# Row maxima of the second attention in pieces of 512 keys, and who adds the weights

## The chip, the cores and the metric

The kernel runs on one core of one Trainium2 chip. The metric is the device time of one execution in microseconds (us); lower is better. The engines of the core are named as in the profile: PE (TensorE, matmuls), PEld (its weight loads), DVE (VectorE), ACT (ScalarE), POOL (GpSimd) and SP (SyncE, which issues DMAs).

## The reference

`x` is 4 x 512 tokens of 256 features and `ctx_1024` is 4 x 1601 context rows of 256 features. Two layers follow each other, each an attention over the context and then a feed-forward part with eight experts. Everything is float32.

```python
x = x + _L0_xattn_ref(ctx_1024, _layernorm(x), ...)      # 8 heads of 128, over context and x
x = x + _L0_ffn_ref(_layernorm(x), ...)                  # 2 of 8 experts a token, limited capacity
x = x + _L1_xattn_ref(ctx_1024, _layernorm(x), Wq, Wk, Wv, 1, 0, 1)
x = x + _L1_ffn_ref(_layernorm(x), ...)                  # 2 of 8 experts a token
```

The third line is what the change touches. It has 8 heads of 32 features, 512 queries and 1601 keys in each of four batches:

```python
q = _split_heads(query @ Wq.T, h)     # query: the normalized x
k = _split_heads(key @ Wk.T, h)       # key, value: the context
v = _split_heads(value @ Wv.T, h)
attn = jnp.einsum('bhnd,bhmd->bhnm', q, k) * scale
attn = jax.nn.softmax(attn, axis=-1)
x = jnp.einsum('bhnm,bhmd->bhnd', attn, v)
```

## The kernel before

The kernel works in four stages, one behind the other: first attention, first experts, second attention, second experts. The second attention is cut into 16 units. A unit `u` is one batch `b`, one group `o` of four heads (`HG` is 4) and one half `f` of the queries, 256 of them. The 1601 keys of a unit make 13 key tiles (`NM`), 12 of 128 keys and one of 65.

A softmax needs the maximum of each row of scores before its exponentials. The kernel therefore computes the scores twice, in two layouts:

- `maxima(u, g)` has queries on the partitions and keys along the row. One call takes 128 queries and a quarter of the keys (400 or 401, `edges`), for all four heads. It takes two tiles of the PSUM pool `ps_s`, writes the scores of two heads into each (L1133), and VectorE reduces each tile to its maxima `tops` (L1141). There are eight calls to a unit: two groups of queries times four quarters.
- `negated(u)` (L1150) reduces `tops` to one negative maximum for each query and head, in `shift`; `to_row(u)` turns it (L1163, PE) and ScalarE copies it as an extra row beside the queries, in `asked` (L1167).
- `weights(u, j)` has the 128 keys of tile `j` on the partitions and queries along the row. Four matmuls (L1180) give the scores, less the maxima through that extra row, in one tile of `ps_s`; ScalarE takes the exponential (L1193) into `pT`.
- `add_weights(u, j, pT)` (L1202) adds that tile to a running sum of the unit. There are two sums. The tiles `j` in `by_pool` are added by GpSimd, the others by VectorE. The first tile of each sum is written by ScalarE straight into the sum's buffer.
- `weigh(u, j, pT, ps)` (L1211) multiplies the weights with the values. `closing` (L1230 on) adds the two sums over the keys, divides and adds the result to `x`.

The loop at the end of the stage takes two key tiles a step and runs over the key tiles of all 16 units, so that steps cross from one unit to the next (13 is odd). The maxima of unit `u` are computed some 18 key tiles ahead, within the steps of the unit before. A step of the kernel before issues, in this order: one call of `maxima` if one is due, `weights` of two key tiles, further calls of `maxima` if due, then `add_weights` and `weigh` for the two tiles of the previous step (`held`), and last what the table `at` has for these key tiles: `negated`, `to_row`, loads of queries and keys, projections for the next batch, layer norms, routing for the second experts. `in_order` ties the instructions of PE, DVE, ACT and POOL to the order in which the program issues them; nothing reorders them. The DMA queue of SP takes its loads as they are issued.

The pools matter here. `ps_s` has three buffers of two PSUM banks each, handed out in turn: whoever asks for a buffer waits until the tile handed out three requests earlier has been read. `pT` has six buffers. With `ps_o` and `ps_m`, one buffer each, this fills the eight banks.

Of the kernel before, what the change touches and what calls it, by code (L numbers as in the profile page):

```python
# [8 lines left out]
F32 = mybir.dt.float32  # L9
# [7 lines left out]
P = 128  # L17
B, S, D = 4, 512, 256
M = 1601
# [9 lines left out]
NM = -(-M // P)  # L29
# [7 lines left out]
H1, DH1 = 8, 32  # L37
HG = P // DH1
# [29 lines left out]
def xattn_ffn_twice(ctx: ExitStack, tc: tile.TileContext, a: dict, out: bass.AP):  # L68
    nc = tc.nc

    @contextmanager
    def in_order(*engines):

        block = nc.cur_bb.bb
        start = len(block.instructions)
        yield
        assert nc.cur_bb.bb is block
        last = {}
        for k, ins in enumerate(block.instructions):
            if ins.engine not in {e.engine for e in engines}:  # L80
                continue
            if k >= start and ins.engine in last:
                tc.add_manual_dep(
                    ins,
                    last[ins.engine].name,
                    mybir.DependencyInfo(
                        mybir.DependencyClass.NoSync, mybir.DependencyReason.DATA
                    ),
                    reason="in_order",
                )  # L90
            last[ins.engine] = ins
# [440 lines left out]
    with ExitStack() as st:  # L532
# [3 lines left out]
        two = st.enter_context(tc.tile_pool(name="a_two", bufs=2))  # L536
# [167 lines left out]
        def values(pair, part):  # L704

            blocks = parts[part]
            v = one.tile([P, len(blocks), 2 * DH0], F32, tag=f"v{part}", name=f"v{part}")
            cols = slice(INNER + pair * 2 * DH0, INNER + (pair + 1) * 2 * DH0)  # L710

            def some(j0):
                n = min(2, len(blocks) - j0)
                ps = ps_t.tile([P, 2, 2 * DH0], F32, tag="t", name="ps_v")
                for k in range(n):
                    j = blocks[j0 + k]
                    for c in range(DC):
                        nc.tensor.matmul(  # L718
                            ps[:, k, :],
                            lhsT=flat_kvin[c][:, j * P : (j + 1) * P],  # L720
                            rhs=wkv[:, c, cols],
                            start=c == 0,
                            stop=c == DC - 1,
                        )
                nc.scalar.copy(v[:, j0 : j0 + n, :], ps[:, :n, :])  # L725

            return v, [lambda j0=j0: some(j0) for j0 in range(0, len(blocks), 2)]
# [72 lines left out]
        for h in range(H0):  # L800
            nc.vector.tensor_copy(values_bias, bqk[:, 2, h : h + 1].to_broadcast([P, P]))
            nc.tensor.matmul(
                ps, lhsT=values_bias, rhs=wo[:, h, :], start=h == 0, stop=h == H0 - 1
# [21 lines left out]
        for n in range(n_steps + 4):  # L825
            b, h, t = n // (H0 * NT), n // NT % H0, n % NT
            if n < n_steps:
                if t == 0:
# [3 lines left out]
                    g = n // NT + 1  # L832
# [5 lines left out]
                if t >= 2 and h % 2 == 0:  # L838
                    v, f = values(h // 2, t - 2)
# [18 lines left out]
            if 1 <= n <= n_steps:  # L858
                p = (n - 1) // 2
# [9 lines left out]
            pieces = []  # L869
# [3 lines left out]
            p = (n - 3 - part) // 2  # L873
# [43 lines left out]
    def keys_values(psum, tag, b, evacuate=evacuate):  # L917


        cT = w1p.tile([P, DC, M], F32, tag="cT", name="cT")  # L920
        nc.sync.dma_start(cT, a["ctxT"][b].rearrange("(c p) m -> p c m", p=P))
        kT = [kv1.tile([P, M], F32, tag=f"kT{o}", name=f"kT{o}") for o in range(DC)]
        v = kv1.tile([P, NM, D], F32, tag="v1", name="v1")

        def some_keys(o, j0):
            n = min(512, M - j0)
            ps = psum.tile([P, 512], F32, tag=tag, name="ps_k1")
            for c in range(DC):
                nc.tensor.matmul(
                    ps[:, :n],  # L930
                    lhsT=wT[:, 1, c, o * P : (o + 1) * P],
                    rhs=cT[:, c, j0 : j0 + n],
                    start=c == 0,
                    stop=c == DC - 1,
                )
            evacuate(kT[o][:, j0 : j0 + n], ps[:, :n])

        def some_values(j0):
            n = min(2, NM - j0)
            ps = psum.tile([P, 2, D], F32, tag=tag, name="ps_v1")  # L940
            r = P
            for k in range(n):
                r = rows_of(j0 + k, NM, TAIL)
                for c in range(DC):
                    nc.tensor.matmul(
                        ps[:r, k, :],
                        lhsT=cT[:, c, (j0 + k) * P : (j0 + k) * P + r],
                        rhs=wT[:, 2, c, :],
                        start=c == 0,
                        stop=c == DC - 1,  # L950
                    )
            evacuate(v[:r, j0 : j0 + n, :], ps[:r, :n, :])

        steps = [lambda j0=j0: some_keys(0, j0) for j0 in range(0, M, 512)]
        steps += [lambda j0=j0: some_values(j0) for j0 in range(0, NM, 2)]
        steps += [lambda j0=j0: some_keys(1, j0) for j0 in range(0, M, 512)]
        return kT, v, steps

    def run(kvs):
        for s in kvs[2]:  # L960
            s()
        return kvs[:2]
# [30 lines left out]
    with ExitStack() as st:  # L993
        two = st.enter_context(tc.tile_pool(name="b_two", bufs=2))
# [11 lines left out]
        kvs = [run(keys_values(ps_h, "h", 0))]  # L1006
# [41 lines left out]
    QH = 2 * P  # L1048
    with ExitStack() as st:
        one = st.enter_context(tc.tile_pool(name="c_one", bufs=1))  # L1050
        two = st.enter_context(tc.tile_pool(name="c_two", bufs=2))
# [46 lines left out]
        qTs = {}  # L1098
# [17 lines left out]
                        qTs[b][i * DH1 : (i + 1) * DH1, o, f * QH : (f + 1) * QH],  # L1116
                    )

        edges = [k * M // HG for k in range(HG + 1)]
        tops = {}  # L1120

        def maxima(u, g):

            b, o, f = units[u]
            t, k = divmod(g, HG)
            if g == 0:
                tops[u] = two.tile([P, 2, HG, HG], F32, tag="tops", name="tops")
            lo, hi = edges[k], edges[k + 1]
            q0 = f * QH + t * P
            pss = [ps_s.tile([P, 2, 512], F32, tag="s", name=f"ps_s{i}") for i in range(2)]  # L1130
            for i in range(HG):
                rows = slice(i * DH1, (i + 1) * DH1)
                nc.tensor.matmul(  # L1133
                    pss[i // 2][:, i % 2, : hi - lo],
                    lhsT=qTs[b][rows, o, q0 : q0 + P],
                    rhs=kvs[b][0][o][rows, lo:hi],
                    start=True,
                    stop=True,
                )
            for pair in range(2):  # L1140
                nc.vector.tensor_reduce(  # L1141
                    tops[u][:, t, 2 * pair : 2 * pair + 2, k],
                    pss[pair][:, :, : hi - lo],
                    AX.X,
                    ALU.max,
                )
# [20 lines left out]
                nc.scalar.copy(asked[u % 3][r : r + 1], ps[r : r + 1])  # L1167


        by_pool = (1, 3, 5, 7, 9, 11)  # L1170
        sums = {}

        def weights(u, j):
# [93 lines left out]
        at = {}  # L1267
# [64 lines left out]
        load_queries(0)  # L1332
        load_keys(0, 1)
        ordered = st.enter_context(in_order(*computing))
        for g in range(2 * HG):
            maxima(0, g)
        negated(0)
        to_row(0)

        ahead = {}  # L1340
        for u in range(1, n_units):
            for g in range(2 * HG):
                step = NM * u - 5 - NM + (g * NM) // (2 * HG)
                ahead.setdefault(max(step, 0) // 2, []).append((u, g))

        held = []
        for step in range(0, NM * n_units + 10, 2):
            first, *more = ahead.pop(step // 2, [None])
            if first:
                maxima(*first)  # L1350
            fresh = []
            for k in range(step, step + 2):
                u, j = divmod(k, NM)
                if u < n_units:
                    fresh.append((u, j, weights(u, j)))
            for g in more:
                maxima(*g)
            for h in held:
                add_weights(*h)
            for uw, jw, pT in held:  # L1360
                if jw == 0:
                    ps_of = ps_o.tile([P, QH], F32, tag="o", name="ps_o1")
                weigh(uw, jw, pT, ps_of)
                if jw == NM - 1:
                    ending = closing(uw, ps_of)
                    next(ending)
                    put(step + 4, lambda ending=ending: next(ending))
                    put(step + 6, lambda ending=ending: next(ending, None))
            for k in range(step, step + 2):
                for f in at.pop(k, []):  # L1370
                    f()
            held = fresh
# [5 lines left out]
    with ExitStack() as st:  # L1378
        one = st.enter_context(tc.tile_pool(name="d_one", bufs=1))
        two = st.enter_context(tc.tile_pool(name="d_two", bufs=2))  # L1380
# [224 lines left out]
        rest = routing()  # L1605
        fetched = [first_tile(0), first_tile(1)]
        more = [lambda e=e: first_tile(e) for e in range(2, E)]
# [41 lines left out]
        with tc.If(ties > 0):  # L1649
            for b in range(B):  # L1650
                for t0 in range(0, NT, GR):
                    rows, acc = [], spare.tile([P, GR, D], F32, tag="acc", name="acc")
# [18 lines left out]
                    for e in range(E):  # L1671
                        t = spare.tile([P, WIDE], F32, tag="w", name="w_t")
# [83 lines left out]
```

## Time and profile before

| | |
|---|---|
| median of 3 runs | 3014.13 us (3011.76 to 3015.57) |
| profiled execution | 3014.63 us, span 3012.6 us, mean granted clock 0.965 |
| busy shares of the span | PE 92%, DVE 48%, ACT 31%, POOL 16% |
| second attention, main loop | about 1985 to 2680 us of the span |
| maxima, reductions L1141 | 256, mean 984 ns |
| weights, scores L1180 | 1664 matmul records |
| weights, exponentials L1193 | 1023 ns each |
| sums on DVE L1202 | 96, mean 1597 ns |
| sums on POOL L1202 | 80, mean 2463 ns |

A row of a group names line, engine, operation, tiles (output <- inputs), shapes and count; then busy time in us, mean ns of one, and the time that the engine stood idle just before such instructions, with what ended it. In a timeline a row has start in us, duration in us, engine, line and operation; in brackets stands the idle time before it and what ended it. Each float32 matmul of the program appears as two records. The ends of matmuls are modelled, so the distance from one start to the next says more than the duration.

### The profile page before, as it was taken

How to read it: one execution, taken by the hardware profiler on the slowest of the kernel's cores; microseconds unless marked ns; L12 is line 12 of the kernel's file. 1: busy time of each engine (PE TensorE's matmuls, PEld its weight loads, DVE VectorE, ACT ScalarE, POOL GpSimd, SP SyncE). 2: the span in 40 equal slices, each digit the busy share in tenths (PEclk: the TensorE clock that was granted, in tenths of full speed). 3: DMA queues.
4: the chain of work that ended last, by engine and by line, in shares of the span. 5: the costliest groups of instructions: out<-in, count | busy, mean ns of one | idle time of the engine just before them, and what ended most of it. 6: DMA issues, size and time to landing. Idle time of an engine off the chain costs nothing. (4 is left out here: it accounts for less than half of the span.)

```text
span 3012.6 us, 35574 instructions
## 1 busy us (share of the span) xinstructions
PE 2781.7 (92%) x13426; PEld 1846.2 (61%) x13426; DVE 1444.5 (48%) x2324; ACT 931.1 (31%) x1312; POOL 473.7 (16%) x340
## 2 busy tenths in 40 slices
PE   5699999999999999999997999788988888898998
PEld 2466676666666667666665566544444444467887
DVE  4256447554476444464444100177775757751110
ACT  2233234232343333332321212123433434341221
POOL 1000000100001000010000100122424434343442
PEclk9899999999999999999998999889999999999999
DMA  8743334433343333333334233210101110045652
GB/s 297 234 123 94 99 92 105 112 96 92 94 113 104 98 86 95 93 102 97 92 96 148 93 98 105 66 27 14 30 26 36 30 35 22 13 172 165 193 171 73
DMA packets 165103, 295.95 MB, mean 98 GB/s; under 512 B 43287, under 2 KB 81752, under 8 KB 161848
## 3 DMA queue, kind: packets, MB, share of 16 engines
q1 hardware_dynamic: 124024, 204.45, 24.2%
q0 software_dynamic: 16320, 53.42, 5.9%
q10 hardware_dynamic: 24576, 35.68, 4.6%
q8 instruction: 109, 1.79, 0.3%
q14 instruction: 74, 0.61, 0.1%
HBM read 97.86 MB, written 49.76 MB: 49 GB/s over the span
## 5 line engine op out<-in xcount | busy, mean ns | idle before, releaser
L743 DVE TENSOR_REDUCE top<-ps_s 128x1 f32<-128x2113 f32 x128 | 301.8, 2358 | 578.9 <-PE ps_s L735 578.9
L772 PE MATMUL ps_o<-pT,v 128*128 128x256 f32 x2176 | 520.9, 381 | 7.8 <-DVE pT L764 7.8
L735 PE MATMUL ps_s<-kT,qT 128*128 128x512 f32 (+1 forms) x1280 | 489.0, 527 | 26.7 <-ACT attn L749 26.3
L772 PEld LDWEIGHTS ps_o<-pT,v 128*128 128x128 f32 x2176 | 410.9, 191 | 124.8 <-issue 69.9
L735 PEld LDWEIGHTS ps_s<-kT,qT 128*128 128x128 f32 x1280 | 241.5, 191 | 276.3 <-issue 239.9
L749 ACT ACTIVATE attn<-ps_s,top 128x2113 f32<-128x2113 f32 x128 | 258.9, 2023 | 486.1 <-DVE top L743 411.5
L764 DVE STREAM_TRANSPOSE pT<-swapped 128x2176 f32<-128x2176 f32 x128 | 312.4, 2441 | 70.2 <-DMA swapped<-attn 59.4
L1141 DVE TENSOR_REDUCE tops<-ps_s 128x2 f32<-128x800 f32 (+1 forms) x256 | 241.0, 984 | 150.7 <-PE ps_s L1133 150.6
L1180 PE MATMUL ps_w<-asked,keyed 64*128 64x256 f32 (+1 forms) x1664 | 243.7, 418 | 45.7 <-DVE tops L1141 39.4
L685 PE MATMUL ps_k<-kvin,wkv 128*128 128x512 f32 (+1 forms) x640 | 261.9, 533 | 5.2 <-ACT kT L692 5.2
L718 PE MATMUL ps_v<-wkv,kvin 128*128 128x256 f32 x1088 | 253.5, 381 | 0.0
L1202 POOL TENSOR_TENSOR sum<-sum,pT 128x1024 f32<-128x1024 f32 x80 | 197.0, 2463 | 334.4 <-ACT pT L1193 243.5
L1180 PEld LDWEIGHTS ps_w<-asked,keyed 64*128 64x128 f32 (+1 forms) x1664 | 150.4, 193 | 155.6 <-DVE tops L1141 79.7
L1193 ACT ACTIVATE pT<-ps_w 128x1024 f32<-128x1024 f32 (+1 forms) x176 | 178.2, 1023 | 195.4 <-PE ps_w L1180 191.8
L718 PEld LDWEIGHTS ps_v<-wkv,kvin 128*128 128x128 f32 x1088 | 204.9, 190 | 32.7 <-issue 3.4
L692 ACT ACTIVATE kT<-ps_k,bqk 128x512 f32<-128x512 f32 (+1 forms) x160 | 97.1, 620 | 268.1 <-DMA swapped<-attn 128.8
L685 PEld LDWEIGHTS ps_k<-kvin,wkv 128*128 128x128 f32 x640 | 116.5, 192 | 81.0 <-issue 67.1
L1202 DVE TENSOR_TENSOR sum<-sum,pT 128x1024 f32<-128x1024 f32 x96 | 153.3, 1597 | 6.2 <-ACT pT L1193 3.0
L725 ACT COPY v<-ps_v 128x512 f32<-128x512 f32 x144 | 79.8, 560 | 226.2 <-PE ps_v L718 154.0
L1445 PE MATMUL ps_h<-xT,w_e 128*128 128x256 f32 x640 | 143.7, 383 | 3.7 <-issue 3.7
L1133 PE MATMUL ps_s<-kT,qT 32*128 32x400 f32 (+1 forms) x1024 | 142.1, 582 | 3.2 <-ACT pT L1193 2.6
L1464 PE MATMUL ps_y<-w_e,hT 128*128 128x256 f32 x640 | 144.4, 385 | 0.0
(261 smaller groups left out, 2635.6 us busy)
## 6 DMA issues: line engine op xcount, KB each, us to landing
swapped<-attn SPq DMA_DIRECT2D x1536, 68.0 KB
swapped<-attn ACTq DMA_DIRECT2D x512, 68.0 KB
rows_b<-empty SPq DMA_DIRECT2D x36, 530.0 KB
w<-in_w_dram SPq DMA_DIRECT2D x16, 1024.0 KB
w_e<-in_wall_dram SPq DMA_DIRECT2D x7, 2052.0 KB
cT<-in_ctxT_dram SPq DMA_DIRECT2D x4, 1601.0 KB
keyed<-kT SPq DMA_DIRECT2D x32, 200.1 KB
ctx_b<-in_ctx_dram SPq DMA_DIRECT2D x4, 1536.0 KB
```

Source lines behind the costliest of these rows:

```text
L685: nc.tensor.matmul(ps[:, :n], lhsT=wkv[:, c, hs], rhs=flat_kvin[c][:, j0 : j0 + n], start=c == 0, stop=c == DC - 1,)
L718: nc.tensor.matmul(ps[:, k, :], lhsT=flat_kvin[c][:, j * P : (j + 1) * P], rhs=wkv[:, c, cols], start=c == 0, stop=c == DC - 1,)
L735: nc.tensor.matmul(flat[:, j0 : j0 + n], lhsT=qT[:, t * P : (t + 1) * P], rhs=kT[:, j0 : j0 + n], start=True, stop=True,)
L743: nc.vector.tensor_reduce(top, flat[:, :L], AX.X, ALU.max, negate=True)
L749: nc.scalar.activation(attn[:, :L], flat[:, :L], AF.Exp, bias=top, accum_out=total)
L764: nc.vector.transpose(pT[:, :, k * P : (k + 1) * P].rearrange("p c (a i) -> p a c i", a=4), swapped.rearrange("p a (c i) -> p a c i", i=32),)
L772: nc.tensor.matmul(ps, lhsT=v[:, j - parts[part][0], (h % 2) * DH0 : (h % 2 + 1) * DH0], rhs=pT[:, j, :], start=j == 0, stop=j == NB - 1,)
L1141: nc.vector.tensor_reduce(tops[u][:, t, 2 * pair : 2 * pair + 2, k], pss[pair][:, :, : hi - lo], AX.X, ALU.max,)
L1180: nc.tensor.matmul(ps[:r, s, pair * QH : (pair + 1) * QH], lhsT=keyed[o][64 * s : 64 * s + 64, pair, j * P : j * P + r], rhs=asked[u % 3][ ...
L1193: nc.scalar.activation(pT[:r], ps[:r], AF.Exp)
L1202: (nc.gpsimd if k else nc.vector).tensor_tensor(to, to, pT[:r], ALU.add)
L1464: nc.tensor.matmul(ps, lhsT=hT[:, f, r * P : (r + 1) * P], rhs=w(WB1 + f * D, D), start=f == 0, stop=f == FC - 1,)
```

## The change

The four quarters of the keys become three pieces of 512 keys, for each of the two groups of 128 queries, and one last piece that holds the remaining 65 keys of both groups side by side. That makes seven calls of `maxima` a unit instead of eight, with the same number of matmuls and of scores; the last call's reduction gives both groups' maxima at once. `tops` keeps its shape, four values a query and head.

In a step, all calls of `maxima` that are due now stand between the scores of the first and of the second key tile; none stands ahead of the first. They are due every second key tile.

GpSimd's tiles become `j` = 1, 4, 7, 10 in place of 1, 3, 5, 7, 9, 11. As the first of each only starts a sum, GpSimd now makes three of the eleven additions of a unit and VectorE eight; before they made five and six.

```diff
-        edges = [k * M // HG for k in range(HG + 1)]
+        rest = M // 512 * 512
+        pieces = [[(t, j0, 512)] for t in range(2) for j0 in range(0, rest, 512)]
+        pieces.append([(t, rest, M - rest) for t in range(2)])
+        n_tops = rest // 512 + 1
         def maxima(u, g):
             b, o, f = units[u]
-            t, k = divmod(g, HG)
...
-            lo, hi = edges[k], edges[k + 1]
-            q0 = f * QH + t * P
             pss = [ps_s.tile([P, 2, 512], F32, tag="s", name=f"ps_s{i}") for i in range(2)]
-            for i in range(HG):
-                rows = slice(i * DH1, (i + 1) * DH1)
-                nc.tensor.matmul(
-                    pss[i // 2][:, i % 2, : hi - lo],
-                    lhsT=qTs[b][rows, o, q0 : q0 + P],
-                    rhs=kvs[b][0][o][rows, lo:hi],
...
+            at = 0
+            for t, j0, n in pieces[g]:
+                q0 = f * QH + t * P
+                for i in range(HG):
+                    rows = slice(i * DH1, (i + 1) * DH1)
+                    nc.tensor.matmul(
+                        pss[i // 2][:, i % 2, at : at + n],
+                        lhsT=qTs[b][rows, o, q0 : q0 + P],
+                        rhs=kvs[b][0][o][rows, j0 : j0 + n],
...
+                at += n
+            t, j0, n = pieces[g][0]
             for pair in range(2):
+                of = pss[pair][:, :, :at].rearrange("p i (t n) -> p t i n", n=n)
                 nc.vector.tensor_reduce(
-                    tops[u][:, t, 2 * pair : 2 * pair + 2, k],
-                    pss[pair][:, :, : hi - lo],
+                    tops[u][:, t : t + at // n, 2 * pair : 2 * pair + 2, j0 // 512],
+                    of,
...
-        by_pool = (1, 3, 5, 7, 9, 11)
+        by_pool = (1, 4, 7, 10)
...
-                step = NM * u - 5 - NM + (g * NM) // (2 * HG)
+                step = NM * u - 6 - NM + 2 * g
                 ahead.setdefault(max(step, 0) // 2, []).append((u, g))
         for step in range(0, NM * n_units + 10, 2):
-            first, *more = ahead.pop(step // 2, [None])
-            if first:
-                maxima(*first)
             fresh = []
             for k in range(step, step + 2):
                 u, j = divmod(k, NM)
                 if u < n_units:
                     fresh.append((u, j, weights(u, j)))
-            for g in more:
-                maxima(*g)
+                if k == step:
+                    for g in ahead.pop(step // 2, ()):
+                        maxima(*g)
             for h in held:
                 add_weights(*h)
```

More of the change, by code (lines that the diff above doesn't have):

```diff
@@ L1117, in load_queries @@
                     )
-        edges = [k * M // HG for k in range(HG + 1)]
+        rest = M // 512 * 512
+        pieces = [[(t, j0, 512)] for t in range(2) for j0 in range(0, rest, 512)]
+        pieces.append([(t, rest, M - rest) for t in range(2)])
+        assert 2 * (M - rest) <= 512
+        n_tops = rest // 512 + 1
         tops = {}
@@ L1124, in maxima @@
             b, o, f = units[u]
-            t, k = divmod(g, HG)
             if g == 0:
-                tops[u] = two.tile([P, 2, HG, HG], F32, tag="tops", name="tops")
-            lo, hi = edges[k], edges[k + 1]
-            q0 = f * QH + t * P
+                tops[u] = two.tile([P, 2, HG, n_tops], F32, tag="tops", name="tops")
             pss = [ps_s.tile([P, 2, 512], F32, tag="s", name=f"ps_s{i}") for i in range(2)]
-            for i in range(HG):
-                rows = slice(i * DH1, (i + 1) * DH1)
-                nc.tensor.matmul(
-                    pss[i // 2][:, i % 2, : hi - lo],
-                    lhsT=qTs[b][rows, o, q0 : q0 + P],
-                    rhs=kvs[b][0][o][rows, lo:hi],
-                    start=True,
-                    stop=True,
-                )
+            at = 0
[7 more added lines that the diff above has]
+                        rhs=kvs[b][0][o][rows, j0 : j0 + n],
+                        start=True,
+                        stop=True,
+                    )
+                at += n
+            t, j0, n = pieces[g][0]
             for pair in range(2):
+                of = pss[pair][:, :, :at].rearrange("p i (t n) -> p t i n", n=n)
                 nc.vector.tensor_reduce(
-                    tops[u][:, t, 2 * pair : 2 * pair + 2, k],
-                    pss[pair][:, :, : hi - lo],
+                    tops[u][:, t : t + at // n, 2 * pair : 2 * pair + 2, j0 // 512],
+                    of,
                     AX.X,
@@ L1334, in xattn_ffn_twice @@
         ordered = st.enter_context(in_order(*computing))
-        for g in range(2 * HG):
+        for g in range(len(pieces)):
             maxima(0, g)
@@ L1341, in xattn_ffn_twice @@
         for u in range(1, n_units):
-            for g in range(2 * HG):
-                step = NM * u - 5 - NM + (g * NM) // (2 * HG)
+            for g in range(len(pieces)):
+                step = NM * u - 6 - NM + 2 * g
                 ahead.setdefault(max(step, 0) // 2, []).append((u, g))
```

## The prediction

> **What bounds the kernel now.** I read first the busy shares by stretch, cut to the second attention (1985 to 2680 us, 16 units), since the diff touches nothing else; then the costliest groups; then the waits of TensorE; then the timeline of a plain step. Nothing is saturated in that stage, as the sum over the stretches shows (695 us):
>
> ```profile
> sum 695.00, PE 599.66 PEld 322.36 DVE 491.35 ACT 281.35 POOL 284.12; mean PE 42.83 PEld 23.03 DVE 35.10 ACT 20.10 POOL 20.29
> ```
>
> TensorE (PE) is nearest to full, with 95 us idle, and VectorE (DVE) is at 71%. The page gives the durations of what the change touches:
>
> ```profile
> L1141 DVE TENSOR_REDUCE tops<-ps_s 128x2 f32<-128x800 f32 (+1 forms) x256 | 241.0, 984 | 150.7 <-PE ps_s L1133 150.6
> L1202 POOL TENSOR_TENSOR sum<-sum,pT 128x1024 f32<-128x1024 f32 x80 | 197.0, 2463 | 334.4 <-ACT pT L1193 243.5
> L1202 DVE TENSOR_TENSOR sum<-sum,pT 128x1024 f32<-128x1024 f32 x96 | 153.3, 1597 | 6.2 <-ACT pT L1193 3.0
> ```
>
> The waits of TensorE in the stage (us, times, longest) name the reduction first:
>
> ```profile
> PE ps_w L1180 <- DVE tops L1141: 39.4, 33, 4.9
> PE ps_c L468 <- DVE earlier L464: 16.7, 3, 5.6
> PE ps_r L1163 <- DVE shift L1150: 15.2, 8, 3.0
> ```
>
> The timeline of a plain step shows why: maxima (M), scores of two key tiles (W0, W1), values of the two tiles before (G).
>
> ```profile
> 2112.28 0.96 PE L1133 MATMUL ps_s<-kT,qT 32*128 32x401 f32 x8
> ...
> 2113.17 2.29 PE L1180 MATMUL ps_w<-asked,keyed 64*65 64x256 f32 x16
> 2113.27 1.89 DVE L1141 TENSOR_REDUCE tops<-ps_s 128x2 f32<-128x802 f32 x2 [2.42 <-PE ps_s L1133]
> ...
> 2114.32 0.73 PEld L1180 LDWEIGHTS ps_w<-asked,keyed 64*128 64x128 f32 x8 [0.53 <-DVE tops L1141]
> ...
> 2115.38 1.07 PE L1211 MATMUL ps_o<-pT,v 128*32 128x256 f32 x16
> ...
> 2116.38 0.95 PE L1133 MATMUL ps_s<-kT,qT 32*128 32x400 f32 x8
> ```
>
> Start to start, M is 0.89 us, W0 with W1 2.21, G 1.00: 4.10 a step. `ps_s` has three buffers and M takes two, so W1 reuses the first buffer of the M just before it, and starts only when that reduction ends (2113.27 + 0.98 = 2114.25, then 2114.32). In the last unit, where no maxima are left, W0 and W1 take 1.88 to 1.93. So even the best step loses 0.3 us there, and any lateness of VectorE is passed on in full. The worst plain case is a step with two maxima (three in 13):
>
> ```profile
> 2100.28 1.14 PE L1180 MATMUL ps_w<-asked,keyed 64*128 64x256 f32 x8 [1.19 <-DVE tops L1141]
> 2101.35 0.95 PE L1133 MATMUL ps_s<-kT,qT 32*128 32x400 f32 x8
> ...
> 2102.34 1.89 DVE L1141 TENSOR_REDUCE tops<-ps_s 128x2 f32<-128x800 f32 x2 [1.21 <-PE ps_s L1133]
> 2102.69 2.34 POOL L1202 TENSOR_TENSOR sum<-sum,pT 128x1024 f32<-128x1024 f32 x1 [3.65 <-ACT pT L1193]
> 2104.14 1.97 DVE L1202 TENSOR_TENSOR sum<-sum,pT 128x1024 f32<-128x1024 f32 x1
> ...
> 2106.25 0.66 PE L1163 MATMUL ps_r<-ident,shift 128*128 128x128 f32 x4 [2.95 <-DVE shift L1150]
> ```
>
> **What the Trainium skill says.** "SBUF — State Buffer", Who interferes with whom: VectorE with two SBUF inputs and a reading GpSimd exclude each other for a whole instruction; a reduction is never affected. The trace agrees: the addition at 2104.14 lasts 1.97 us because GpSimd's runs to 2105.04, others last 1.21, while reductions stay between 923 and 996 ns. "TensorE: Matmul & The Clock Gate", What's actually happening: the clock halves after idle windows of about 3.4 us. In the stage's stretches PEclk means 0.936, so some 89 us ran at half clock, costing about 44. "TensorEngine Tiling", Key Properties: a change of tiling mode drains the array. M, W and G have three modes, and the new order W M W G has four changes a step for three; no row prices one alone.
>
> **The change part by part.** Times are from W0's start.
>
> *Sizes.* A reduction of 1,024 elements: L1141 gives 984 ns at 800 and L743 2358 at 2113, so 1.046 ns an element and 1.22 us; the piece of 260 comes to 0.42. Per unit 12 x 1.22 + 2 x 0.42 = 15.5 us against 16 x 0.984 = 15.7: nothing, and the 16 reductions of the prologue likewise. Matmuls: L685 at 512 columns costs 261.9/640 = 409 ns, L718 at 256 costs 253.5/1088 = 233, so 0.69 ns a column; M of 512 is 0.89 + 2 x 112 x 0.69 ns = 1.04 us. The last piece, 16 short instructions, is unseen: between 0.3 (by columns) and 0.9 (by count); I take 0.5.
>
> *Order.* W0 [0, 0.96], M [0.96, 2.0]. W1 now reuses W0's buffer, so it needs ScalarE's exponential: scores start to exponential start is 1.18 in the timeline (2117.27 to 2118.45), plus 1.02, plus 0.06 to start: W1 at 2.26, 0.26 later than TensorE could. W1 takes 1.06 (2114.32 to 2115.38), G 1.00: a step of 4.32. Reductions start at 2.1; issued behind each other they take 1.13 each (the pair above takes 1.89 for 2 x 0.98), so they end at 4.5. Who waits: the next W0 (at 4.32) needs the first, done at 3.3; the next M (at 5.28) needs the second, done at 4.5. VectorE may be about 0.8 us late at no cost, where it now may not be late at all. Per 13 steps (two units, 16 maxima before, 14 after, one step holding two): before 10 x 4.10 + 3 x 4.99 = 56.0; after 13 x 4.32 + 1.0 = 57.2. Eight pairs: **+10 us**.
>
> *Waits removed.* After a two-maxima step VectorE does four reductions and an addition (3.6 + 1.13) from 1.0 on, with a gap for the second matmuls, so it is free at about 7.0 and the next W1 starts 0.9 us late: 24 such steps, **-22**. The ps_o wait of GpSimd's second sum (j=3 comes two steps after j=1, whose matmul still reads that buffer) makes it collide with VectorE and TensorE then loses about 2.3 us in each of three batches; with j=4 it is not late: **-7**. Of some 45 us by which the timeline's W1 and M come late at full clock, these leave 16, which follow layer-norm and collecting work on VectorE; the new slack takes half, **-8**. The wait for `shift` (15.2 us, 8 times): the new step has one M, and VectorE ends reductions, an addition and `shift` at 5.9 against G's end at 4.3, so 1.6 a time: **-2**.
>
> *Sums.* GpSimd 80 to 48, VectorE 96 to 128. Unblocked 1.21 each: +39 us of VectorE, less about a third of the 36 us (96 x 0.38) now lost to the lock: 491 to some 520 of 695, and a step holds 2.26 + 1.23 x 1.13 = 3.65 us of 4.32. GpSimd's 79 us are off the path. An addition starts at 4.4. GpSimd's starts at 2.4 when its tile is the step's first (ends 4.7, little harm), but at 4.6 when it is the second; VectorE is ahead by 0.2 us, unless late. After the steps with two additions before j=7 or 10 it is late: it then waits for the lock to 6.9, and TensorE loses about 0.8. Two in 13 steps: **+13**.
>
> *ScalarE.* The six square roots, each with two table loads of 1.28 us ahead of an exponential, could so far hide; now W1 waits for them. Bounds 0 and 2.5 each; I take 1.5: **+9**. No DMA is moved, and SP's and ScalarE's orders stay as they are.
>
> *Clock.* The stalls of 2 to 3 us become shorter ones; if a fifth of the half-clock time goes, **-8**. Bounds: -20, and +10 if many short gaps count as idleness.
>
> Sum: 10 - 22 - 7 - 8 - 2 + 13 + 9 - 8 = **-15**. The profiled execution took 3014.6 us (span 3012.6); the median is 3014.1, half a microsecond less. So 2999.
>
> **The rivals.** *VectorE becomes the bound through the lock (slower).* If VectorE loses the race for the lock in all three second-place steps of 13, 24 times, and the delay of 2.3 us is not caught up, since only 0.67 us a step are free, TensorE loses about 1.6 each time: +38 where I put +13, and the clock gains nothing (0 for -8): -15 + 25 + 8 = +18, about 3032. It decides once VectorE is over 0.2 us late at its addition. For it: VectorE's additions average 1597 ns against 1210 already. Against it: 32 fewer GpSimd sums. *The exponential holds W1 (no change).* If each W1 comes 0.1 us later than worked out, by ScalarE's copies, that is 104 x 0.1 = +10 and with the table loads at 2.5 another +6: 3015, within the noise. *The clock stays up (faster still).* With -20 for the clock and no collisions: about 2974. That the order is not as stated can be excluded: the built program has W0, M, W1, G.
>
> **How the numbers follow.** A measurement of this kernel can tell about 0.2%, 6 us. Forecast (-30 to -6) 0.40, still faster 0.14, no change 0.14, slower 0.32. The forecast's own range is 2984 to 3008. Leaving out a tenth at each end, with -20 for the clock at one end and the lock with late exponentials at the other, gives 2970 to 3036.
>
> **What would show it.** Right: TensorE's wait for `tops` (39.4 us) falls below 20 and moves to the first W and to M; `pT` or `sum` of L1193 appears as a releaser of the scores' matmuls; reductions of 1.22 us; VectorE's additions at some 1.4 us x128; PEclk above 0.94 in the stage. Wrong: VectorE over 540 us in the stage, additions above 1.6 us, a stage longer than 695 us, or PEclk below 0.92.

## The result and the profile after

The changed kernel takes **2996.0 us** (median of 5, 2988.93 to 2997.69) against 3014.1; the ratio is 0.9938, 95% interval 0.9925 to 0.995, so 18 us or 0.6% faster. The profiled execution took 2993.9 us (span 2992.2) against 3014.6. The scores L1188 run from 1980.9 to 2641.8 us, before (as L1180) from 1985.4 to 2664.8: the main loop of the second attention takes 661.0 us where it took 679.4: 18 of the 20 us by which the two spans differ. (Line numbers move: L1133 is now L1138, L1141 L1149, L1180 L1188, L1193 L1201, L1202 L1210.)

The costliest groups on the page of the changed kernel, for the lines that were shown of before:

```profile
L1149 DVE TENSOR_REDUCE tops<-ps_s 128x2 f32<-128x1024 f32 (+1 forms) x224 | 237.4, 1104 | 135.2 <-PE ps_s L1138 135.0
L1210 DVE TENSOR_TENSOR sum<-sum,pT 128x1024 f32<-128x1024 f32 (+1 forms) x128 | 181.0, 1414 | 10.7 <-ACT pT L1201 3.9
L1210 POOL TENSOR_TENSOR sum<-sum,pT 128x1024 f32<-128x1024 f32 x48 | 124.1, 2585 | 345.7 <-ACT pT L1201 345.5
```

The reductions cost the same in all (237 us for 241), in pieces of 1218 ns, and 422 ns for the small one. VectorE has 32 additions more, yet each is shorter: 1414 ns for 1597. Fewer additions on GpSimd are not enough to explain that, as the sums alone show below.

The waits of TensorE in the stage (us, times, longest):

```profile
PE ps_r L1171 <- DVE shift L1158: 16.0, 6, 4.4
PE ps_w L1188 <- DVE tops L1149: 9.5, 6, 4.1
...
PE ps_s L1138 <- ACT kT L936: 6.8, 2, 3.6
PE ps_w L1188 <- ACT pT L1201: 6.2, 13, 1.3
```

The wait for the reduction went from 39.4 to 9.5 us, and ScalarE is a new releaser of the second scores. A plain step in the timeline (start, duration) shows where each group now stands:

```profile
2104.00 1.08 PE L1188 MATMUL ps_w<-asked,keyed 64*65 64x256 f32 x8
...
2105.02 1.14 PE L1138 MATMUL ps_s<-kT,qT 32*128 32x512 f32 x8
2105.16 1.02 ACT L1201 ACTIVATE pT<-ps_w 65x1024 f32<-65x1024 f32 x1 [1.01 <-PE ps_w L1188]
...
2106.23 1.13 PE L1188 MATMUL ps_w<-asked,keyed 64*128 64x256 f32 x8
2106.76 2.35 DVE L1149 TENSOR_REDUCE tops<-ps_s 128x2 f32<-128x1024 f32 x2
...
2107.30 1.07 PE L1219 MATMUL ps_o<-pT,v 128*32 128x256 f32 x16
...
2108.30 1.13 PE L1188 MATMUL ps_w<-asked,keyed 64*128 64x256 f32 x8
```

The exponential of the first tile ends at 2106.18, and the second scores start 0.05 us later, 2.23 after the first. The reductions start 0.6 us late here (VectorE had two additions before them) and nobody waits. The step takes 4.30 us.

### The profile page after: what moved, and what is told of

It reads as the page before. It is cut to its first block, busy times and chain, and to the rows that moved or that the text cites. A ratio compares the mean times of both kernels' runs of the same rounds, so it can differ in the third digit from the quotient of the medians.

```text
span 2992.2 us, 35534 instructions
## 1 busy us (share of the span) xinstructions
PE 2778.0 (93%) x13426; PEld 1839.3 (61%) x13426; DVE 1456.4 (49%) x2324; ACT 933.3 (31%) x1312; POOL 400.0 (13%) x308
## 4 chain that ended last, share of the span: by engine, by line
PE 82%; DVE 7%; issue 3%; DMA 3%; ACT 3%; SPq 2%; POOL 1%; POOLq 0%; DVEq 0%; ACTq 0%
PE ps_o L772 15%; PE ps_s L735 15%; PE ps_v L718 7%; PE ps_k L685 7%; PE ps_w L1188 6%; PE ps_y L1470 4%; PE ps_h L1451 4%; PE ps_h L970 4%; PE ps_y L983 4%; DVE tops L1149 2%; PE ps_o L1219 2%; DVE sum L1210 2%; PE ps_p L783 2%; PE ps_v L945 2%; PE ps_q L670 2%
## 5 line engine op out<-in xcount | busy, mean ns | idle before, releaser
L1149 DVE TENSOR_REDUCE tops<-ps_s 128x2 f32<-128x1024 f32 (+1 forms) x224 | 237.4, 1104 | 135.2 <-PE ps_s L1138 135.0
L1188 PE MATMUL ps_w<-asked,keyed 64*128 64x256 f32 (+1 forms) x1664 | 244.2, 415 | 20.5 <-DVE tops L1149 9.5
L1201 ACT ACTIVATE pT<-ps_w 128x1024 f32<-128x1024 f32 (+1 forms) x176 | 179.5, 1024 | 192.5 <-PE ps_w L1188 190.4
L1188 PEld LDWEIGHTS ps_w<-asked,keyed 64*128 64x128 f32 (+1 forms) x1664 | 147.0, 189 | 143.2 <-ACT pT L1201 60.7
L1210 DVE TENSOR_TENSOR sum<-sum,pT 128x1024 f32<-128x1024 f32 (+1 forms) x128 | 181.0, 1414 | 10.7 <-ACT pT L1201 3.9
L1210 POOL TENSOR_TENSOR sum<-sum,pT 128x1024 f32<-128x1024 f32 x48 | 124.1, 2585 | 345.7 <-ACT pT L1201 345.5
L1138 PE MATMUL ps_s<-kT,qT 32*128 32x512 f32 (+1 forms) x1024 | 140.5, 577 | 12.5 <-ACT kT L936 6.8
```

Of the source, the lines that this page charges most:

```text
L1149: nc.vector.tensor_reduce(tops[u][:, t : t + at // n, 2 * pair : 2 * pair + 2, j0 // 512], of, AX.X, ALU.max,)
L1188: nc.tensor.matmul(ps[:r, s, pair * QH : (pair + 1) * QH], lhsT=keyed[o][64 * s : 64 * s + 64, pair, j * P : j * P + r], rhs=asked[u % 3][ ...
L1210: (nc.gpsimd if k else nc.vector).tensor_tensor(to, to, pT[:r], ALU.add)
```

## The experiments

Times are medians, beside those of before on the same chip (3012 to 3015 us); differences in us come from the ratios.

**One part, or two, at a time.** The change has three parts: pieces, order, sums. The sums alone:

```diff
-        by_pool = (1, 3, 5, 7, 9, 11)
+        by_pool = (1, 4, 7, 10)
```

> Only GpSimd's tiles change, from 1,3,5,7,9,11 to 1,4,7,10; maxima and order stay as before. Theory A (the order gives VectorE slack, the sums cost a little): VectorE has 32 more additions of 1.13 us to pass, in a step that tolerates no lateness, less a third of the lock's losses and less the late second sum: -5 to +12 us against before, most likely +3. Theory B (the gain comes from GpSimd's additions no longer locking VectorE out): about -15 us, the whole gain of the change. Theory C (all comes from fewer, larger pieces): 0.

Measured 3044.8, ratio 1.0102 (1.0085 to 1.0118): **31 us slower**, beyond every theory. TensorE's wait for the reductions, 39.4 us before, grew:

```profile
PE ps_w L1180 <- DVE tops L1141: 63.1, 40, 5.4
```

The stage from first to last scores shows the busy times of PE, PEld, DVE, ACT and POOL, then PEclk; first before, then this kernel:

```profile
1985.00:2665.00 680.00, 588.63 (x4978) 314.64 (x4974) 481.33 (x756) 277.62 (x332) 276.38 (x148) 0.94 0.10 26
```

```profile
1985.00:2697.00 712.00, 604.45 (x4974) 321.57 (x4972) 519.50 (x786) 277.65 (x332) 200.68 (x117) 0.92 0.09 25
```

VectorE has 38 us more to do, and the stage is 32 us longer. Up to 19 us of that is the clock: by the clock records of the two traces 119 us of the stage ran at half clock, where it was 82 before. Nor did VectorE's additions become shorter, though GpSimd makes fewer beside them:

```profile
L1202 DVE TENSOR_TENSOR sum<-sum,pT 128x1024 f32<-128x1024 f32 (+1 forms) x128 | 206.0, 1609 | 10.4 <-ACT pT L1193 3.9
```

An addition that nothing blocks takes 1.21 us here. Above that, these 128 lose 51 us, where the 96 of before lost 37.

The pieces alone keep the old place in the step and the old sums:

```diff
+        pieces = [[(t, j0, 512)] for t in range(2) for j0 in range(0, rest, 512)]
+        pieces.append([(t, rest, M - rest) for t in range(2)])
...
-                step = NM * u - 5 - NM + (g * NM) // (2 * HG)
+                step = NM * u - 5 - NM + (g * NM) // len(pieces)
```

> Only the pieces change (seven of 512 keys a unit, in before's place ahead of the scores of both tiles; GpSimd keeps 1,3,5,7,9,11). Theory A: the second tile's scores now wait for a reduction of 1.22 instead of 0.98 us (+0.24 x 96 = +23 us), with two steps of 13 fewer that hold two pieces (-14 to -20): 0 to +10 us. Theory B: 0. Theory C: -15 us.

Measured 2996.6, ratio 0.994 (0.9926 to 0.9954): **18 us faster**, as much as the whole change. Theory C's number is right and A's wrong. What I had expected to be lost is there: the second scores wait for the longer reduction, more often and for as long in all as before.

```profile
PE ps_w L1188 <- DVE tops L1149: 41.6, 73, 3.5
```

The waits listed are many and short where they were few and long (33, the longest 4.9). In a plain step of before the second scores are late too, but by too little for the list: they start 1.15 us after the first, and 0.97 us after where nothing holds them. And the stage ran at a better clock:

```profile
1982.00:2638.00 656.00, 571.32 (x4982) 306.45 (x4982) 477.30 (x726) 276.88 (x331) 276.84 (x148) 0.96 0.10 27
```

From 0.94 to 0.96 is some 4% of 680 us at half clock less, 27 us, of which half is time: 14 us of the 24 by which the stage shrank in the profiles. The profiled execution is the fastest of the six (2987.5 us), but the better clock is in all of them: over the whole kernel 0.968 to 0.971, against 0.964 to 0.968 before.

The order alone:

```diff
-            first, *more = ahead.pop(step // 2, [None])
-            if first:
-                maxima(*first)
...
-            for g in more:
-                maxima(*g)
+                if k == step:
+                    for g in ahead.pop(step // 2, ()):
+                        maxima(*g)
```

> Only the order changes: all pieces of a step stand between the scores of its two tiles; eight pieces of 400 keys a unit, GpSimd keeps 1,3,5,7,9,11. Theory A: a gain, cut by the three steps in 13 with two pieces, where the second piece and the second scores wait for reductions (about 1.5 us more each, 24 times, against the 0.9 us saved): -5 to -15 us. Theory B: 0. Theory C: 0 or slower.

Measured 3011.6, ratio 0.9993 (0.9985 to 1.0001): no change. The wait for the reduction has all but gone here too, but the second scores now wait for the exponential, 0.3 us in each of 53 places:

```profile
PE ps_w L1180 <- ACT pT L1193: 16.0, 53, 0.5
...
PE ps_s L1133 <- ACT pT L1193: 6.2, 21, 0.6
PE ps_s L1133 <- DVE tops L1141: 6.1, 4, 3.2
PE ps_w L1180 <- DVE tops L1141: 5.8, 6, 2.4
```

In a step with two pieces they stand behind both, and such a step takes 6.0 us in this trace, where it took 5.0. In exchange the step after it is not late: its second scores start 2.28 us after the first (median of 17 such steps at full clock), as in the other steps of this order. Before, they started 2.03 us after the first (median of nine such steps), elsewhere 1.15. The order thus removes the lateness and pays for it one step earlier. The runs had a better clock than those of before (medians 0.968 and 0.965 over the whole kernel), so at an equal clock this kernel would probably be slower than before.

Pieces and order, with the old sums (the change with `by_pool = (1, 3, 5, 7, 9, 11)`):

> The change with before's sums (GpSimd keeps 1,3,5,7,9,11). Theory A: most of the gain, with more meetings of GpSimd's and VectorE's additions but fewer additions on VectorE: -8 to -22 us against before, within 8 us of the full change. Theory B: near 0. Theory C: -15.

Measured 3002.4, ratio 0.9964 (0.9951 to 0.9978): 11 us faster than before. It is within the range of theory A. The change's own sums bring another 8 us or less (0.9938; the intervals all but touch). The clock has a part in that: its median over the whole kernel is 0.964 in these runs and 0.968 in those of the change.

Pieces and sums in the old order (the pieces alone with `by_pool = (1, 4, 7, 10)`):

> Pieces of 512 and GpSimd's tiles 1,4,7,10, in before's order (pieces ahead of the scores of both tiles). Theory A: the two additions more a unit cost here what they cost alone in the old order, about +30 us on top of the pieces' -18: +5 to +25 us against before. Rival (the sums do harm only together with the eight pieces): -15 to -25.

Measured 3033.6, ratio 1.0074 (1.0046 to 1.0101): 22 us **slower**, as theory A had it, and 40 us more than the pieces alone. With the runs before it this makes a table (ratio to before):

| | old sums | new sums |
|---|---|---|
| 400 keys, old order | 1 | 1.0102 |
| 512 keys, old order | 0.9940 | 1.0074 |
| 400 keys, new order | 0.9993 | not run |
| 512 keys, new order | 0.9964 | 0.9938 |

The same edit of the sums costs 31 to 40 us in the old order and nothing, or a gain, in the new one. That is what the order does: it does not make the kernel faster by itself, it lets VectorE take more work.

How much of these differences is the clock can be estimated from the profiled executions, one of each kernel, from the first scores to the last. Eight matmul records of L1188 that take 1.13 us take 2.08 at half clock (at 2362.19 in the changed kernel), so the clock cost at most half of the time at half clock. The last column is what VectorE's additions lost in all above 1.21 us each (all in us):

| | stage | of it at half clock | stage less half of that | lost by additions |
|---|---|---|---|---|
| before | 679 | 82 | 639 | 37 |
| sums | 712 | 119 | 652 | 51 |
| pieces | 655 | 54 | 628 | 31 |
| order | 675 | 62 | 645 | 31 |
| pieces and order | 665 | 79 | 625 | 55 |
| pieces and sums | 696 | 85 | 653 | 50 |
| all three | 661 | 72 | 625 | 26 |

With the clock taken out this way, the pieces bring about 10 us and the order costs about 6 when alone. The sums cost about 14 and 25 us in the old order and nothing in the new one. The last column says why in part: GpSimd's three additions a unit hold VectorE up more than five did in the old order and less in the new one, so it matters where they fall and not only how many they are.

**How late VectorE may be.** One more reduction ahead of each call's two, of scores that are reduced again at once:

```diff
+            nc.vector.tensor_reduce(
+                tops[u][:, t, 0:2, k], pss[0][:, :, :192], AX.X, ALU.max
+            )
             for pair in range(2):
```

> The kernel before, with one reduction more ahead of each call's two (384 scores of the first tile, reduced once more to the same place and then overwritten), which makes VectorE about 0.46 us later in every call, 128 calls, 59 us of VectorE. Theory A (in the old order the second scores wait directly for the reduction, so lateness is passed on in full): +45 to +60 us, and more if the clock falls. Rival (only VectorE's total load counts): no more than the same edit costs in the changed kernel.

> The changed kernel with the same extra reduction ahead of each call's two (384 scores, 260 in the last piece), 112 calls, about 50 us of VectorE. Theory A (the next scores need that reduction only 0.8 to 1 us after it is due): +5 to +20 us against the changed kernel. Rival (only the total load counts, and VectorE is fuller here): +45 us or more.

Measured: in the kernel before, 3095.0, ratio 1.0275 (1.0248 to 1.0303), 83 us slower. In the changed kernel, 3039.9, ratio 1.009 (1.0062 to 1.0117), some 45 us slower than that kernel. VectorE's busy time in the stage grew by 60 us in the one (481 to 541) and 55 in the other (494.5 to 549). So the new order passes on about 0.8 of what VectorE is late, the old one 1.4 (1.2 if the stage of the profiled execution is taken, 72 us longer, in place of the medians). Its tolerance is real, but smaller than the 5 to 20 us of theory A would mean; the rival's "45 or more" fits its own number, though not its claim that the old kernel would lose no more. In the changed kernel the clock fell with it:

```profile
1989.00:2692.00 703.00, 610.19 (x4976) 319.04 (x4978) 549.18 (x862) 279.11 (x332) 191.56 (x117) 0.92 0.09 25
```

Its stage grew by 42 us in the profiles, and 106 us of it ran at half clock for 72: up to 17 of the 42 us are the clock. In the kernel before it is up to 6 of 72. With the clock taken out, the new order passes on about half of the lateness.

**What the pieces gain by.** Two runs place the seven pieces of 512 otherwise, in the old order with the old sums:

```diff
-                step = NM * u - 5 - NM + (g * NM) // len(pieces)
+                step = NM * u - 6 - NM + 4 * (g // 2)
```

> Pieces of 512 in before's order and with before's sums, but due two at a time, every fourth key tile, so that half of all steps hold two pieces instead of one in 13. Theory A2 (the pieces gain because fewer steps hold two, after which VectorE is late): seven two-piece steps in 13 at 0.9 us each and more: the gain of 18 us is gone, +10 to +40 us against before. Rival (fewer, larger reductions are cheaper for TensorE's modes or the clock): still -10 to -20.

Measured 2993.5, ratio 0.9936 (0.9913 to 0.9958): as fast as the pieces alone, although six of 13 steps hold two pieces (one of them three). The expectation left out that each is followed by a step with none, in which VectorE catches up. So two pieces in a step do not cost by themselves. The next run has them followed by a step with one:

```diff
+                step = NM * u - 6 - NM + (0, 0, 2, 6, 6, 8, 12)[g]
```

> Pieces of 512 in before's order and with before's sums, but due so that a unit's seven pieces fall into its steps as 2, 1, 0, 2, 1, 0, 1: four steps in 13 hold two pieces and are followed by a step with one. Theory A2 (what costs is a two-piece step followed at once by another piece, since VectorE then ends its fourth reduction and addition at 8.1 us where the next piece is ready at 6.7): 1.3 us each, some 30 times, less what the empty steps save: +20 to +45 us on the pieces alone, so 0 to +27 us against before. Rival (seven pieces are cheaper in themselves, wherever they stand): -10 to -20 us, as for the pieces alone and the paired ones.

Measured 3005.2, ratio 0.9979 (0.9968 to 0.999): 12 us slower than the pieces alone, so the following piece matters, but the gain is not all gone. In the trace the second scores behind a two-piece step start 2.26 us after the first (median of 19 such steps at full clock), in a plain step of the pieces alone 1.39: 0.9 us late and not 1.3. Over some 30 places that would be 26 us, of which the empty steps probably give back about half. Neither theory holds in full. Eight pieces need three two-piece steps in 13, seven need one; that explains part of the pieces' gain. Another part is the clock: up to 14 of 24 us in the profile of the pieces alone, up to 7 of 23 in that of the paired ones. How much each brings, and whether larger pieces are cheaper in themselves, is not settled.

**ScalarE in the way.** In the changed kernel the longest stall of a piece is this one; the lines are of ScalarE, VectorE and TensorE, shortened to those in question:

```profile
2354.16 1.28 ACT L132 ACT_TABLE_LOAD   x1
...
2359.74 0.17 DVE L130 TENSOR_SCALAR ve<-mv 128x4 f32<-128x4 f32 x1
...
2359.94 0.20 ACT L132 ACTIVATE rs<-ve 128x4 f32<-128x4 f32 x1 [4.50 <-DVE ve L130]
2360.05 0.20 ACT L936 COPY kT<-ps_k 128x65 f32<-128x65 f32 x1
...
2360.30 1.96 PE L1138 MATMUL ps_s<-kT,qT 32*128 32x512 f32 x4 [3.57 <-ACT kT L936]
2361.56 1.02 ACT L1201 ACTIVATE pT<-ps_w 65x1024 f32<-65x1024 f32 x1
```

ScalarE stands at a layer norm's square root, waiting 4.5 us for VectorE's variance; behind it are a copy whose buffer the next piece needs and the exponential that the second scores need. In all (first before, then after):

```profile
ACT rs L132 <- DVE ve L130: 8.0, 5, 1.7
```

```profile
ACT rs L132 <- DVE ve L130: 18.7, 6, 4.5
```

The test issues the root one step after the variance:

```diff
         mv = ln_moments(two, xb, n)
-        root = ln_root(two, mv, n)
+        ve = ln_var(two, mv, n)
         yield
+        root = ln_root(two, mv, n, ve)
+        yield
```

> The changed kernel with the square root of the two layer norms issued one step after the variances (VectorE's mean and variance stay where they are), so that ScalarE does not stand waiting for VectorE's variance with a copy and the next exponential queued behind it. Theory A (in the new order the second scores and the next piece wait for ScalarE: 4 to 5.7 us at four places of the trace, about 1.5 at two or three more, of which 1.7 each remain for the two table loads): -8 to -18 us against the changed kernel. Rival (VectorE is late at those places in any case, so the wait moves to the reductions): within 4 us of the changed kernel.

Measured 2985.9, ratio 0.9901 (0.9886 to 0.9917): **11 us faster than the changed kernel**, as theory A had it. The wait of `rs` for `ve` is no longer in the list. In the profiles the stage is 16 us shorter, and 52 us of it ran at half clock for 72, so up to 10 of the 16 us are the clock. The root was not set apart in the kernel before; how much of this cost the change itself brought is not shown.

**Further along the same list.** The transposes of `shift` one key tile later, and then also the routing's choice cut by two yields:

```diff
-            put(NM * u - 4, lambda u=u: to_row(u))
+            put(NM * u - 3, lambda u=u: to_row(u))
```

> The changed kernel with the square root apart, and with the transposes of the maxima (to_row) issued one key tile later, so that in no unit they stand in the step in which VectorE still makes them. The waits of ps_r for shift (13 us in 7 places with the root apart) should be gone. Theory A (TensorE's own waits are the cost, and the next scores wait for nothing of these): -6 to -15 us against the kernel with the root apart. Rival (VectorE's backlog is the limit and the wait moves to the next scores): within 4 us of it.

```diff
         nc.vector.tensor_copy(pay[:, :, D + 1 :], wb)
+        yield
...
+        yield
         ps = psum.tile([P, n, E], F32, tag=tag, name="ps_c2")
```

> As the one before, and the routing's long chain of small VectorE operations (some 10 us in one step, at three places, where ps_c waits 19 us in all) cut into three steps. Theory A: TensorE works on while VectorE catches up by at most 4 us a step: -8 to -18 us on top of the later row. Rival (VectorE's backlog is the limit): within 4 us of the kernel with the later row.

Measured 2975.7, ratio 0.9879 (0.9858 to 0.99), and 2970.2, ratio 0.9867 (0.9842 to 0.9891). The later row brings some 7 us on top of the root, within theory A's range, though the two intervals overlap. The split brings about 4 more, inside the noise of the two intervals and below the 8 to 18 expected; it is what the rival forecast. Of the 18.9 us that TensorE waits there with the later row, 11.5 remain:

```profile
PE ps_c L474 <- DVE earlier L470: 18.9, 3, 6.3
```

```profile
PE ps_c L476 <- DVE tops L1159: 11.5, 3, 4.0
```

By the ratios, the last kernel is 40 us faster than before and 21 faster than the changed one.

## Why the prediction came out right, and where its steps did not

The forecast was 2999 us and the sign was right. The sum of -15 us met a measured -18, but its terms were off both ways, so that the number is this close is partly luck. Most of the signs named for it came: TensorE's wait for the reduction fell to 9.5 us, the exponential appears as a releaser, reductions take 1.22 us, additions 1.41, and PEclk is above 0.94.

*Sizes and order of a step.* The reduction of 1,024 elements was to take 1.22 us and takes 1.218; the small one 0.42 and takes 0.422. The second scores were to start at 2.26 us and start at 2.23; the step of 4.32 takes 4.30. This step of the prediction holds to a hundredth, because each number came from a start-to-start distance in a plain step.

*Waits removed, -22.* The lateness after a two-piece step was sized rightly, 0.9 us, and the order does remove it. But I credited the order with the gain, and this step failed: the two-piece step itself becomes 1 us longer in the new order, so the order alone gives 0.9993. What takes the lateness away at a profit is that seven pieces leave 7 such steps where there were 21, in either order; the pieces alone give 0.9940. In the sum the two parts stood together, so its total did not suffer.

*Sums, +13.* Wrong in the order in which they stand: with the new order they cost nothing and bring up to 8 us. The lock's part was right for the change as a whole: what VectorE's additions lose above 1.21 us fell from 37 to 26 us in all (128 x 0.204 against 96 x 0.387), the third that I had taken off. That it falls with GpSimd's count was wrong: with the same sums in the old order it rose to 51 and 50 us. VectorE's busy time grew by 13 us in the stage's windows (481 to 494.5), not by 29: the additions alone by 28, as worked out, but the reductions and other operations became shorter by some 14 us. GpSimd's wait for `ps_o`, 90.5 us before, is no longer among its long waits; with the sums alone it was still 112 us, so the new tiles alone do not remove it.

*ScalarE, +9.* The engine was right and the reason was not. I charged two table loads at six places; the larger cost is ScalarE's wait for the variance (18.7 us for 8.0), with the piece and the exponential queued behind it. Taking it away gave 11 us, but part of that wait was there before, so the size of the term is not shown.

*The wait for shift, -2.* It did not fall: 15.2 us became 16.0, in six places where it was eight. The likely reason, which no run tests alone: the step with one piece is shorter for TensorE too, so TensorE is there earlier and VectorE, with more additions, later.

*Clock, -8.* PEclk over the stage went from 0.94 to 0.95. Unrounded, 72 us of it ran at half clock for 82, worth up to 5 us.

```profile
1981.00:2642.00 661.00, 590.25 (x4982) 310.22 (x4982) 494.53 (x757) 279.56 (x332) 205.39 (x117) 0.95 0.10 27
```

*The rival with the lock.* It did not come about here, but the sums in the old order came out at 3045 and 3034 us, and the first has two of the signs that were named for being wrong: a stage of 712 us and additions of 1.61 us. So the lock probably takes part there. The rest is probably the order: the additions stand ahead of the reduction for which the second scores wait.

## What to carry to other kernels

Ask of each engine's queue what stands directly behind a result that the busiest engine waits for: moving the consumer one buffer later gained nothing by itself here, but it turned an edit that cost 31 us into one that does no harm. An in-order engine that waits for another engine's small result, as ScalarE did for a variance, holds up everything behind it; issuing the consumer one step after the producer is cheap and gave more than any single part of the change but the pieces. When parts are changed together, run each alone: here one part gave the whole gain, one gave none, and one was harmful unless the order went with it. And before a difference of 10 us is given a cause, look at how long each kernel ran at half clock.

## What the runs showed of the hardware that was not expected

The granted clock multiplies stalls. With the same number of matmuls and of columns in the stage, PEclk was 0.96 with the pieces alone, 0.94 before and 0.92 with the sums alone or with late reductions in the changed kernel; 0.02 is about 14 us in a stage of 680. It does not follow the total of waiting: with late reductions TensorE is idle for 150 us in the kernel before and for 93 in the changed one, and the first has the better clock, 0.94 against 0.92.

The traces show what it follows. Each gives the clock in windows of 3.41 us, at full or at half speed. Taken over this stage in all 14 traces, after a window at full clock: where TensorE was idle for 2 us or more of the window, the next one ran at half clock in 127 of 127 cases; where it was idle for less than 1 us, in 13 of 2,091. After a window at half clock, 0.75 us of idleness was enough to stay there (62 of 62). Two stretches of the kernel before, cut at these windows (PE busy is the first figure after the length, PEclk the one after POOL):

```profile
2128.44:2131.85 3.41, 1.36 (x16) 0.75 (x16) 3.41 (x4) 1.02 (x1) 2.20 (x2) 1.00 0.00 0
2131.85:2135.26 3.41, 3.41 (x34) 1.44 (x32) 1.47 (x1) 1.02 (x1) 0.39 (x1) 0.50 0.02 5
...
2480.01:2483.42 3.41, 2.00 (x26) 0.73 (x24) 2.37 (x3) 1.02 (x1) 2.01 (x1) 1.00 0.00 0
2483.42:2486.83 3.41, 1.86 (x16) 1.10 (x18) 1.85 (x4) 1.15 (x2) 2.11 (x2) 1.00 0.07 25
2486.83:2490.24 3.41, 3.39 (x40) 1.74 (x36) 2.73 (x3) 2.05 (x2) 0.23 (x1) 1.00 0.00 0
```

In the first, 2.05 us of idleness in one window halves the clock of the next. In the second, 1.41 and 1.55 us in two windows, more in all, cost only themselves. The prediction took it that a window has to be idle; more than half of one was enough. So what counts is how much of a stall falls into one window. Many short waits, as with the pieces alone, seldom reach that, and where a stall of 2 us falls is partly chance.
